# One transposed form of the tokens for both attentions, and router logits from columns of two products, in a transformer block with two attentions and a mixture of experts

## The chip, the cores and the metric

The kernel runs on one core of one Trainium2 chip. The metric is device time in microseconds (us). The engines are PE (TensorE; PEld is its weight load), DVE (VectorE), ACT (ScalarE), POOL (GpSimd) and SP, which here only issues DMAs. Each engine takes its own instructions in the order of the program, and a semaphore holds an instruction back until what it needs is done.

## The reference

The input is x, 32 sequences of 256 tokens of 128 numbers, in float32. The parts that matter:

```
xn = layernorm(x)                                   # no weights
q, k, v = xn @ Wq, xn @ Wk, xn @ Wv                 # attention A: 16 heads of 8, over the 256 tokens
scores = (qc @ kc.T + q_var * k_var) / D            # centred q and k, and their variances
a = softmax(scores) @ v @ Wo
hn = layernorm(xn) * ln1_w + ln1_b                  # attention B: over the 32 sequences, causal
qkv = hn @ in_proj_w.T + in_proj_b
attn = softmax_causal(q @ k.T / sqrt(8)) @ v @ out_proj_w.T + out_proj_b
x1 = xn + attn
hn2 = layernorm(x1) * ln2_w + ln2_b
rp = softmax(hn2 @ router_w.T)                      # 8 experts, the best two
y = sum over the two of gate * gelu(hn2 @ w1[e]) @ w2[e]
out = x + a + x1 + y
```

Note that xn is a layernorm of x, and that hn normalises xn once more: its mean is already zero, and its scale differs from one only through the epsilon. The factor between the two is one number for each token, called r2 in the code.

## The kernel before, in words

**First phase (first_rounds, last_rounds).** Attention B and the router run in 16 chunks of 512 tokens: a chunk is 16 positions of all 32 sequences, as four tiles (k) of 128 tokens. The loop `for i in range(-2, NCHUNK)` works on several chunks at once: turn_in and project_in for chunk i + 2, scores for i + 1, weigh for i, project_out for i - 1, the logits for i - 2. The order of the calls is the order of the instructions on each engine (`manual_schedule`); nothing reorders them.

The steps that the change or the prediction touches:
- load (L140) brings a chunk, in runs of four tokens (2 KB); up to seven chunks are resident.
- stats (L257) takes mean and variance of four tiles on VectorE (L262, L263) and the reciprocal square root on POOL (L265, L266). measure (L269) calls it for the chunk i + 4 and goes on with six small POOL instructions (L274 to L280); the last is r2.
- norms (L288) writes xn to `zx` on ScalarE (L291), and POOL multiplies by r2 for zn (L295).
- turn_in (L303) transposes both xn (pta, into `xnT`, for attention A) and zn (ptb, into hT with ln1's weights, for attention B). POOL then adds the output bias to zx (L311).
- project_in (L313) makes keys (pk, L316), queries (pq, L322) and values (pv, L327), which ScalarE copies out (kb L320, qT L324, v L328). The values go through DRAM (`vald`) and come back in another arrangement (spread, L334).
- scores, lessened (L374, L375 on VectorE: maximum and subtraction, four groups), exponents (L378), turn_weights (ptp, L383), weigh (L395), divide (L412, L413) are the softmax and its product with the values.
- turn_out (pto, L417) and project_out (px, L424): VectorE adds px to zx for x1 (L426) and takes its statistics; POOL adds x1 to the residual (L429), which goes to DRAM (L431). normalise (L433) on POOL writes hn2 without its weights into zx.
- turn_normed and logits (L440 to L449) transpose this once more (ptc), apply ln2's weights, and multiply by the router's matrix (pl) into `lg`.
- set_second (L221) clears tiles on POOL in rounds 3 to 5.

PSUM has two pools of four banks each; a bank is free for the fourth allocation after it.

**Second phase.** Attention A goes in units of 8 steps (step, L942); each sequence's q, k and v come from project (pp, L557), which reads `xnT` with a stride of 32. Beside the first half runs route (L717): the instructions of the softmax over experts and of the positions are handed out a few a step (some, L931), then 128 indirect DMAs of POOL scatter the tokens to their experts' blocks (L801). Then come the experts (L870), and the second half of attention A with the gathering of their results (L894).

The diff touches these functions:

Of the kernel before, what the change touches and what calls it, by code (L numbers as in the profile page):

```python
# [68 lines left out]
def block_kernel(  # L69
# [26 lines left out]
    xv = x.rearrange("s (i c k) e -> i c s (k e)", c=4, k=4)  # L96
# [7 lines left out]
    xnT = cp.tile([P, NCHUNK, 512], F32, name="xnT")  # L104
# [14 lines left out]
    rv = resd.rearrange("s (i c k) e -> i c s (k e)", c=4, k=4)  # L119

    vec = cp.tile([P, 7], F32, name="vec")
    l1w, l1b, l2w, l2b = (vec[:, n:n + 1] for n in range(4))
# [5 lines left out]
    mhalf = cp.tile([P, 4, 1], F32, name="mhalf")  # L128
    wqkv = cp.tile([P, 3, P], F32, name="wqkv")
    wo = cp.tile([P, P], F32, name="wo")  # L130
    inT = cp.tile([P, 3, P], F32, name="inT")
    outT = cp.tile([P, P], F32, name="outT")
    rT = cp.tile([P, NE], F32, name="rT")

# [5 lines left out]
    def load(i):  # L140
        xt = ax.tile([P, 4, P], F32, tag="xt", name=f"xt{i}")
        for c in range(4):
            nc.sync.dma_start(xt[32 * c:32 * c + 32].rearrange("s k e -> s (k e)"), xv[i, c])
        return xt
# [13 lines left out]
    late = xnT[:, NCHUNK - 2:NCHUNK].rearrange("p i t -> p (i t)").rearrange("p (n m) -> p n m", m=P)  # L158
    ipw, opw, qkw, rw, bvs = late[:, 0:3], late[:, 3], late[:, 4:6], late[0:NE, 6], late[:, 7]
    qkT, ccen = zx[:, NTILE - 2:NTILE], zx[:, NTILE - 3]  # L160

    def loads():
# [7 lines left out]
        nc.scalar.dma_start(opw, out_proj_w)  # L170
        nc.scalar.dma_start(bout, out_proj_b.partition_broadcast(P))
# [3 lines left out]
        nc.sync.dma_start(rw, router_w)  # L175
# [5 lines left out]
    def set_in():  # L181
        nc.vector.tensor_scalar(bk4, cst[:, C_M4:C_M4 + 4], bk, None, ALU.mult)
        pt = bank_u([P, 4, P], "pt0")
        for n in range(3):
            nc.tensor.transpose(pt[:, n, :], ipw[:, n, :], ident)
        nc.tensor.transpose(pt[:, 3, :], opw, ident)
        nc.vector.tensor_copy(inT[:, 0:2, :], pt[:, 0:2, :])

        nc.vector.tensor_copy(
            inT[:, 2, :].rearrange("p (j g d) -> p j g d", j=4, g=4),  # L190
            pt[:, 2, :].rearrange("p (g j d) -> p j g d", j=4, g=4),
        )
        nc.vector.tensor_copy(outT, pt[:, 3, :])
# [7 lines left out]
    def set_rest():  # L201
        pt = bank_w([P, 4, P], "pt1")
        nc.tensor.transpose(pt[:, 0, :], qkw[:, 0, :], ident)
        nc.tensor.transpose(pt[:, 1, :], qkw[:, 1, :], ident)
        nc.tensor.transpose(pt[:, 2, 0:NE], rw, ident[0:NE, 0:NE])
        nc.vector.tensor_copy(qkT, pt[:, 0:2, :])
        nc.vector.tensor_copy(rT, pt[:, 2, 0:NE])
# [3 lines left out]
        nc.vector.tensor_copy(wqkv[:, 0:2, :], pb)  # L211

# [42 lines left out]
    xts, rss, nrm, mvs, zns, hTs, qTs, kbt, scs, prs, pTs, wps, os, oTs, x1s, h2s = ({} for _ in range(16))  # L255
# [198 lines left out]
    def first_rounds():  # L454
# [9 lines left out]
        for i in range(-2, NCHUNK):  # L464
# [48 lines left out]
            if chunk(i - 2):  # L513
                turn_normed(i - 2)
# [506 lines left out]
```

## Time and profile before

The time before is 1243.65 us, the median of 15 runs (1237.62 to 1249.68).

| | |
|---|---|
| profiled execution, its own time | 1243.08 us |
| its span, first to last instruction | 1240.9 us |
| mean granted TensorE clock | 0.895 |
| PE, PEld busy | 1014.7, 707.2 us |
| DVE, ACT, POOL busy | 707.8, 659.6, 562.2 us |
| packets of all DMAs | 87,747, of 76.32 MB |

In time: the first phase lasts to about 285 us, its rounds some 14 us each; attention A's first half runs at about 8.5 us a unit until 392; from 392 to 564 all engines but POOL are nearly still, while POOL scatters (384 to 547); then attention A goes on to 742, the experts run until 885, and attention A's second half with the gathering until the end.

How to read the lines: a row of a timeline gives the start, the busy time, the engine, the line of the kernel, the operation, what is written and read, the shape and the count; in brackets stands how long the engine was idle before it, and what released it. PE's rows can overlap, since matmuls are pipelined. A row of stages gives, for each engine, its busy time and in brackets its instructions.

### The profile page before, as it was taken

What the parts mean: (1) busy time and instruction counts of PE and PEld (TensorE: products, weight loads), DVE (VectorE), ACT (ScalarE), POOL (GpSimd) and SP (SyncE); (2) the same over time, 40 slices, a digit from 0 to 9 for tenths busy, and PEclk for the clock granted to TensorE, in tenths of its full rate; (3) what the DMA queues carried; (4) which work ended last, traced back from release to release, by engine and by line L of the source; (5) the groups of instructions that cost most, each with busy time, mean ns of one, the idle gap of its engine ahead of it and who ended that gap; (6) DMA issues with size and microseconds to landing.
All of it is one profiled execution on the core that took longest, in us unless ns stands there. A gap on an engine that the chain in (4) does not pass through costs nothing.

```text
span 1240.9 us, 32300 instructions
## 1 busy us (share of the span) xinstructions
PE 1014.7 (82%) x13107; PEld 707.2 (57%) x13107; DVE 707.8 (57%) x1638; ACT 659.6 (53%) x1362; POOL 562.2 (45%) x725
## 2 busy tenths in 40 slices
PE   5888999889997211008999999999889989899998
PEld 3667777666664000005666659999645555556665
DVE  2576777579996000006888864444455555557883
ACT  4777788736664000004666665555444544446664
POOL 6488887540004777740000003333578888884000
PEclk8898999999998555557999999999979988999999
DMA  3344443203001611110000004444122211110000
GB/s 92 121 136 129 138 136 90 61 20 102 2 2 33 101 52 52 52 63 1 2 2 2 2 13 130 133 133 137 60 64 66 69 37 56 56 52 16 23 10 14
DMA packets 87747, 76.32 MB, mean 61 GB/s; under 512 B 32840, under 2 KB 70864, under 8 KB 87600
## 3 DMA queue, kind: packets, MB, share of 16 engines
q1 hardware_dynamic: 74736, 48.03, 13.7%
q0 software_dynamic: 11600, 26.10, 6.5%
q8 instruction: 103, 1.69, 0.6%
q14 instruction: 44, 0.36, 0.1%
q10 hardware_dynamic: 1264, 0.14, 0.1%
HBM read 33.98 MB, written 40.24 MB: 60 GB/s over the span
## 4 chain that ended last, share of the span: by engine, by line
PE 67%; another core or an unknown queue 15%; DVE 7%; issue 4%; POOL 3%; ACT 3%; DMA 1%; DVEq 0%; SPq 0%; ACTq 0%; POOLq 0%
PE sm L610 19%; PE pav L634 10%; PE pe L854 5%; PE ph L845 5%; PE pp L557 5%; PE sT L616 4%; PE pqk L584 2%; PE pt L653 2%; PE ptp L300 2%; DVE pr L375 1%; PE sc L359 1%; PE px L834 1%; DVE mt L622 1%; DVE mx L374 1%
## 5 line engine op out<-in xcount | busy, mean ns | idle before, releaser
L622 DVE TENSOR_REDUCE mt<-sm 128x2 f32<-128x512 f32 x512 | 329.3, 686 | 295.3 <-remote 190.9
L625 ACT ACTIVATE ex<-sT 128x512 f32<-128x512 f32 x512 | 279.4, 595 | 358.2 <-PE sT L616 160.1
L610 PE MATMUL sm<-ka,qa 32*128 32x256 f32 x2048 | 324.8, 417 | 77.8 <-DVE mt L622 61.0
L616 PE MATMUL sT<-qa,ka 32*128 32x256 f32 x2048 | 323.1, 415 | 48.8 <-issue 40.0
L610 PEld LDWEIGHTS sm<-ka,qa 32*128 32x128 f32 x2048 | 190.0, 191 | 168.2 <-DVE mt L622 88.9
L616 PEld LDWEIGHTS sT<-qa,ka 32*128 32x128 f32 x2048 | 192.4, 191 | 63.7 <-issue 47.7
L634 PE MATMUL pav<-ex,va 128*32 128x256 f32 x2048 | 160.3, 395 | 37.8 <-issue 37.1
L859 POOL DMA_DIRECT2D ysd<-ye x71 | 47.2, 665 | 290.4 <-issue 200.2
L801 POOL DMA_INDIRECT xsd<-zx,posi x128 | 123.2, 963 | 81.3 <-DVE posi L789 42.7
L905 POOL DMA_INDIRECT yg<-ysd,posb x128 | 122.5, 957 | 43.0 <-issue 30.9
L634 PEld LDWEIGHTS pav<-ex,va 128*32 128x32 f32 x2048 | 58.4, 111 | 118.3 <-issue 83.1
L854 PEld LDWEIGHTS pe<-w,ge 128*128 128x128 f32 x568 | 74.5, 191 | 4.2 <-ACT ge L847 0.7
L854 PE MATMUL pe<-w,ge 128*128 128x128 f32 x568 | 74.9, 275 | 0.3 <-ACT ge L847 0.3
L845 PE MATMUL ph<-xT,w 128*128 128x256 f32 x284 | 73.2, 380 | 0.0
L557 PE MATMUL pp<-wqkv,xnT 128*128 128x384 f32 x128 | 67.7, 611 | 5.0 <-issue 4.2
L858 DVE COPY ye<-pe 128x256 f32<-128x256 f32 x71 | 30.1, 424 | 53.5 <-PE pe L854 53.5
L837 ACT ACTIVATE xT<-px,vec 128x256 f32<-128x256 f32 x71 | 40.0, 564 | 36.9 <-PE px L834 36.9
L920 POOL TENSOR_TENSOR res<-res,yg 128x256 f32<-128x256 f32 x64 | 46.6, 728 | 26.8 <-issue 22.0
L374 DVE TENSOR_REDUCE mx<-sc 128x16 f32<-128x512 f32 x64 | 43.4, 678 | 18.8 <-PE sc L359 18.8
L847 ACT ACTIVATE ge<-ph 128x512 f32<-128x512 f32 x71 | 42.4, 597 | 21.0 <-PE ph L845 21.0
L643 ACT COPY oa<-pav 128x256 f32<-128x256 f32 x64 | 24.1, 377 | 55.1 <-remote 44.1
L378 ACT ACTIVATE pr<-pr 128x1024 f32<-128x1024 f32 x32 | 33.9, 1058 | 36.4 <-DVE pr L375 36.4
(170 smaller groups left out, 1670.6 us busy)
## 6 DMA issues: line engine op xcount, KB each, us to landing
xb<-xsd SPq DMA_DIRECT2D x71, 128.0 KB
ysd<-ye POOLq DMA_DIRECT2D x71, 128.0 KB
xsd<-zero SPq DMA_DIRECT2D x10, 852.0 KB
vald<-v SPq DMA_DIRECT2D x16, 288.0 KB
vb<-vald SPq DMA_DIRECT2D x64, 72.0 KB
xt<-in_L_attn_x_dram SPq DMA_DIRECT2D x64, 64.0 KB
resd<-xt SPq DMA_DIRECT2D x64, 64.0 KB
res<-resd SPq DMA_DIRECT2D x32, 128.0 KB
```

What stands on the lines that cost most here:

```text
L374: nc.vector.tensor_reduce(mx, s, AX.X, ALU.max)
L557: nc.tensor.matmul(pp.rearrange("p n m -> p (n m)"), xs_all[:, ti * P:(ti + 1) * P, s], wqkv.rearrange("p n m -> p (n m)"), start=True, st ...
L610: nc.tensor.matmul(sc[:, i, :], qas[u][r:r + 32, i * P:(i + 1) * P], kas[u][r:r + 32, h, :], start=True, stop=True,)
L616: nc.tensor.matmul(sc[:, i, :], kas[u][r:r + 32, h, i * P:(i + 1) * P], qas[u][r:r + 32, :], start=True, stop=True,)
L622: nc.vector.tensor_reduce(mts[y // 8 % 2][:, :, o:o + 1], sc, AX.X, ALU.max, negate=True)
L625: nc.scalar.activation(exs[y], sc, AF.Exp, scale=1.0 / HD)
L634: nc.tensor.matmul(pos[u][32 * j:32 * j + 32, :], vaugs[s % NV][:, ti, 4 * j + 2 * g + h, :], exs[8 * u + 4 * h + j][:, ti, :], start=(h = ...
L801: yield nc.gpsimd.indirect_dma_start(xsd_views[n * NTILE + k], bass.IndirectOffsetOnAxis(ap=posi[:, k, n:n + 1], axis=0), zx[:, k, :], None,)
L845: nc.tensor.matmul(ph[:, f, :], wb[n][0][:, f * P:(f + 1) * P], xT, start=True, stop=True)
L854: nc.tensor.matmul(pe[:, j, :], ge[:, f, j * P:(j + 1) * P], w2b[:, f, :], start=(f == 0), stop=(f == 1))
L859: nc.gpsimd.dma_start(ysd[n * BLK:(n + 1) * BLK].rearrange("(p j) h -> p j h", j=2), ye)
L905: yield nc.gpsimd.indirect_dma_start(yg[s][:, ti, n, :], None, ysd, bass.IndirectOffsetOnAxis(ap=gt["posb"][:, s, ti, n:n + 1], axis=0),)
```

## The change

A transposed copy of zn alone (`znT`) serves both attentions. ln1's weight goes into the projection's weights (inT, inV) and ln1's bias into in_proj's bias. Attention A would need xn; it takes zn instead and multiplies the products by 1 / r2 for each token, `rall`, when it copies them out of PSUM. rall is made by a reciprocal at the end of measure, and is brought into attention A's order of tokens by a transposition and a way through DRAM (scale_back).

The logits no longer take a transposition and product of their own. With P the router's matrix times ln2's weight, the logits are linear in x1, and x1 is xn plus the attention's output plus a bias: the values' product gets eight more columns (zn times P, then times rall), the output's product gets eight more (out_proj times P), and the rest (mean, bias, scale) is put right once for all tokens, by five POOL instructions at the head of route. normalise still writes zx, now half on POOL and half on VectorE. The tiles hold tokens in another order: load and the residual's writes go in runs of one token (512 B), and the positions' and gates' writes in runs of two numbers.

The diff, cut to its core:

```diff
-    xv = x.rearrange("s (i c k) e -> i c s (k e)", c=4, k=4)
+    xv = x.rearrange("s (i k c) e -> i c s k e", c=4, k=4)
...
-    rv = resd.rearrange("s (i c k) e -> i c s (k e)", c=4, k=4)
+    rv = resd.rearrange("s (i k c) e -> i c s k e", c=4, k=4)
...
     def set_in():
-        nc.vector.tensor_scalar(bk4, cst[:, C_M4:C_M4 + 4], bk, None, ALU.mult)
...
-        nc.vector.tensor_copy(inT[:, 0:2, :], pt[:, 0:2, :])
+        pr = bank_u([P, NE], "ptr")
+        nc.tensor.transpose(pr, rw, ident[0:NE, 0:NE])
+        nc.vector.tensor_scalar(inT, pt[:, 0:2, :], l1w, None, ALU.mult)
+        nc.vector.memset(inV[:, 4, :], 0.0)
+        nc.vector.tensor_scalar(
+            inV[:, 0:4, :].rearrange("p j (g d) -> p j g d", g=4),
             pt[:, 2, :].rearrange("p (g j d) -> p j g d", j=4, g=4),
+            l1w, None, ALU.mult,
         )
+        nc.vector.tensor_copy(rT, pr)
+        nc.vector.tensor_scalar(rP, rT, l2w, None, ALU.mult)
+        nc.vector.tensor_tensor(ipb, ipw, l1bs.unsqueeze(1).to_broadcast([P, 3, P]), ALU.mult)
+        nc.vector.tensor_reduce(bz, ipb, AX.X, ALU.add)
+        nc.vector.tensor_tensor(vec[:, 4:7], vec[:, 4:7], bz.rearrange("p n o -> p (n o)"), ALU.add)
+        nc.vector.tensor_scalar(bk4, cst[:, C_M4:C_M4 + 4], bk, None, ALU.mult)
...
     def measure(i):
...
         nc.gpsimd.tensor_tensor(r2, r2, mhalf, ALU.pow)
+        nc.vector.reciprocal(rall[:, 4 * i:4 * i + 4], r2.rearrange("p k o -> p (k o)"))
...
     def turn_in(i):
-        nc.scalar.copy(
-            xnT[:, i, :].rearrange("p (c k s) -> p k c s", c=4, k=4),
-            transposed(tokens(i), "a", i).rearrange("p (k c s) -> p k c s", k=4, c=4),
-        )
-        hTs[i] = a2.tile([P, 512], F32, tag="hT", name=f"hT{i}")
-        nc.scalar.activation(hTs[i], transposed(zns.pop(i), "b", i), AF.Identity, bias=l1b, scale=l1w)
+        nc.scalar.copy(znT[:, i, :], transposed(zns.pop(i), "b", i))
...
     def project_in(i):
...
-        pv = bank_u([P, 4, 4, 32], f"pv{i}")
-        for k in range(4):
-            nc.tensor.matmul(pv[:, :, k, :], hT[:, k * P:(k + 1) * P], inT[:, 2, :], start=True, stop=True)
-        nc.scalar.copy(
-            vs[i % 2].rearrange("p j k g d -> p (j k g) d")[:, :, 0:HD],
-            pv.rearrange("p j k (g d) -> p (j k g) d", d=HD),
-        )
+        for h in range(2):
+            pv = bank_u([P, 5, 2, 32], f"pv{i}_{h}")
+            for k in range(2):
+                o = (2 * h + k) * P
+                nc.tensor.matmul(pv[:, :, k, :], zT[:, o:o + P], inV, start=True, stop=True)
+            nc.scalar.copy(
+                v[:, :, 2 * h:2 * h + 2].rearrange("p j k g d -> p j (k g) d")[:, :, :, 0:HD],
+                pv[:, 0:4].rearrange("p j k (g d) -> p j (k g) d", d=HD),
+            )
+            t = slice(4 * i + 2 * h, 4 * i + 2 * h + 2)
+            nc.vector.tensor_tensor(
+                lg[:, t, :], pv[:, 4, :, 0:NE], rall[:, t].unsqueeze(2).to_broadcast([P, 2, NE]), ALU.mult
+            )
...
     def project_out(i):
...
+        for h in range(2):
+            px = bank_w([P, 2, P + NE], f"px{i}_{h}")
+            for k in range(2):
+                o = (2 * h + k) * P
+                nc.tensor.matmul(px[:, k, :], oT[:, o:o + P], outX, start=True, stop=True)
+            nc.vector.tensor_tensor(
+                x1[:, 2 * h:2 * h + 2, :], px[:, :, 0:P], tokens(i)[:, 2 * h:2 * h + 2, :], ALU.add
+            )
+            l = lg[:, 4 * i + 2 * h:4 * i + 2 * h + 2, :]
+            nc.vector.tensor_tensor(l, l, px[:, :, P:P + NE], ALU.add)
...
-    def normalise(i, eng=nc.gpsimd):
+    def normalise(i, n=2):
...
         for k in range(4):
+            eng = nc.gpsimd if k < n else nc.vector
...
-    def turn_normed(i):
...
-    def logits(i):
...
+    def scale_back():
+        pr = bank_u([NTILE, P], "pra")
+        nc.tensor.transpose(pr, rall, ident)
+        ra = a1.tile([NTILE, P], F32, tag="ra", name="ra")
+        nc.vector.tensor_copy(ra, pr)
+        nc.sync.dma_start(rnd.rearrange("(n c) s -> n (c s)", c=4), ra)
+        nc.sync.dma_start(rpos[:, 0], rnd.rearrange("(i t) s -> t i s", t=P))
+        nc.vector.tensor_scalar(rpos[:, 1], rpos[:, 0], 1.0 / math.sqrt(HD - 1), None, ALU.mult)
...
-            if chunk(i - 2):
-                turn_normed(i - 2)
...
-            if chunk(i - 2):
-                logits(i - 2)
+            if i == NCHUNK - 3:
+                scale_back()
...
-        nc.scalar.activation(sq, pqk, AF.Square, scale=1.0 / math.sqrt(HD - 1))
+        nc.scalar.activation(sq, pqk, AF.Square, scale=rpos[:, 1, ti, s:s + 1])
...
-        nc.scalar.copy(qk[:, :, 0:HD], pqk)
+        nc.scalar.activation(qk[:, :, 0:HD], pqk, AF.Identity, scale=rpos[:, 0, ti, s:s + 1])
...
     def route():
...
+        yield nc.gpsimd.tensor_tensor(
+            t, mvall[:, :, 0:1].to_broadcast(all8), rows[:, 1:2, :].to_broadcast(all8), ALU.mult
+        )
+        yield nc.gpsimd.tensor_tensor(lg, lg, t, ALU.subtract)
+        yield nc.gpsimd.tensor_tensor(lg, lg, rows[:, 0:1, :].to_broadcast(all8), ALU.add)
+        yield nc.gpsimd.tensor_tensor(lg, lg, rsall.to_broadcast(all8), ALU.mult)
+        yield nc.gpsimd.tensor_tensor(lg, lg, rows[:, 2:3, :].to_broadcast(all8), ALU.add)
         yield nc.vector.tensor_reduce(m, lg, AX.X, ALU.max)
...
-            dv = dram.rearrange("s (i c k) u -> c s i (k u)", c=4, k=4)
+            dv = dram.rearrange("s (n c) u -> c s n u", c=4)
```

## The prediction

> **What bounds the kernel now.** I read the page's busy times first, then the busy time by stage, then one round of the first phase in order of time with the chain of waits beside it, and last the later stages. By stage (start:end, then length, PE, PEld, DVE, ACT, POOL busy, granted clock, DMA share, GB/s):
>
> ```profile
> 116.00:172.00 56.00, 52.61 (x1283) 41.08 (x1282) 40.76 (x119) 47.12 (x81) 45.82 (x72) 1.00 0.42 130
> ...
> 570.00:742.00 172.00, 170.46 (x2119) 107.98 (x2112) 137.95 (x291) 114.30 (x271) 0.00 (x0) 0.98 0.01 2
> ```
>
> The first line is four rounds of the first phase. PE looks like the bound (52.6 of 56), and the change takes matmuls away. But a busy share does not say what ends a round. One round in order of time does:
>
> ```profile
> 161.83 0.69 DVE L426 TENSOR_TENSOR x<-px,zx 128x512 f32<-128x512 f32 x1 [2.94 <-PE px L424]
> ...
> 164.34 0.23 POOL L265 TENSOR_SCALAR rsc<-mvc 128x4 f32<-128x4 f32 x1 [2.18 <-DVE mvc L263]
> ...
> 165.75 0.18 DVE L263 BATCH_NORM_AGGREGATE mva<-sta 128x2 f32<-128x6 f32 x1
> ...
> 165.85 0.66 DVE L374 TENSOR_REDUCE mx<-sc 128x16 f32<-128x512 f32 x1
> ...
> 166.91 1.04 POOL L295 TENSOR_TENSOR zn<-zx,r 128x512 f32<-128x512 f32 x1
> ...
> 167.92 0.23 POOL L265 TENSOR_SCALAR rsa<-mva 128x4 f32<-128x4 f32 x1
> ...
> 170.72 1.04 POOL L280 TENSOR_TENSOR r<-r,mhalf 128x4 f32<-128x4 f32 x1
> ...
> 171.14 0.42 DVE L413 TENSOR_TENSOR o<-po,aden 128x256 f32<-128x256 f32 x1
> ...
> 174.56 1.16 PE L424 MATMUL px<-outT,oT 128*128 128x128 f32 x8
> ...
> 175.83 0.69 DVE L426 TENSOR_TENSOR x<-px,zx 128x512 f32<-128x512 f32 x1 [2.94 <-PE px L424]
> ```
>
> From L426 at 161.83 to L426 at 175.83 is one round, 14.0 us, and the chain of waits runs through it without a gap: VectorE alone from 161.83 to the end of L413 at 171.57 (x1, stats, four softmax groups, two divides), then PE 171.62 to 175.72 (half of pto, pk, pq, pv, px). Call the end of L413 **D**. VectorE's order is the program's: the last stats(i+4) ends at 165.75, its very next instruction is L374. And POOL finishes r, the last value of measure, only at 170.72 + 1.04 = 171.76, because it waits for mvc (164.24), and then has rsc, xt and zn ahead of rsa. Today nothing on VectorE waits for r.
>
> The second attention (second stage line) is PE back to back, 170.5 of 172.
>
> **The change part by part.**
>
> *The wait.* The diff puts a VectorE reciprocal of r2 at the end of measure(i+4). It is queued right behind stats(i+4) and ahead of normalise, both lessened(i+1, 0..1), divide and the rest of the round. The source, r2, is 7.52 us behind the end of mvc (164.24 to 171.76); stats(i+4) cover 1.69 of these. So VectorE stands idle about 5.8 us a round, in the middle of the chain that already sets the round. Who waits behind it: exp of those scores on ScalarE, ptp and pto on PE, and through px the next round.
>
> New round, measured from D:
> - D to the end of px: 4.15 today. pv has 160 columns for 128 (0.89 x 160/128: +0.22), px 136 for 128 (+0.06). 4.43.
> - x1 in two halves (a 128x256 add from PSUM follows in 0.34 by L413; before 0.72 for the whole), lg adds 0.10 each by L449, stats: mvc ends at 6.75 (today 6.67). The lg multiplies and the first half fall into the 2.94 that VectorE waits for px.
> - POOL to r: +7.52 = 14.27. zn also needs ScalarE's norms, which end 9.19 after D (180.76); pv copied in two pieces adds 0.10, still a tie with xt.
> - reciprocal 0.2, two normalise (now VectorE) at 0.27 (L436's four there took 1.15): 15.05.
> - from L374 at 165.85 to 171.57: 5.72, less lg's copy 0.10. Next D at 20.7.
>
> So 20.7 us with a warm PE, not 14.0. On top, PE goes idle: after weigh its next work, ptp, needs the exp of scores that come late, a hole of some 7 us. The row for such a hole (start, busy, then idle before):
>
> ```profile
> 245.88 2.08 PE L424 MATMUL px<-outT,oT 128*128 128x128 f32 x8 [2.50 <-ACT oT L417]
> 247.75 1.68 PE L300 MATMUL ptp<-cst,pr 128*128 128x128 f32 x8
> 249.26 1.03 PE L347 MATMUL sc<-causalb,identb 128*128 128x512 bf16 x4
> ```
>
> px takes 2.08 for 1.06: half clock for 3.4 us. In the start-up the same lasts from 38.14 to 44.0, 5.9 us. In the new round ptp starts 1.85 before D; half clock to 1.55 after D costs the pto-pk-pq-pv-px leg 0.75, half clock to 4.15 after D costs 2.05. The two rows differ and the hole is of neither's length, so I take the middle: 1.35. **Round: 22.0 us** (20.7 to 22.7).
>
> [...]
>
> *Rounds 1 to 11.* Before: first L374 of round 0 at 48.22, that of round 11 at 209.41: 161.2. After: 11 x 22.0, plus set_second's memsets, which stand between xt and zn on POOL (91.73 to 94.20 twice, 124.88 to 126.00 once: 6.1). 248.1. **+87.**
>
> *Start.* In set_in VectorE gets nine more instructions of 0.1 to 0.55 and waits for pbo before measure(1); by rows of like shape 2.6 us, and POOL (start-up's chain) passes it on. Round -1: lessened(0,0) came at 34.25; now it waits for r of chunk 3, 39.6 + 2.6, so 42: +7.8. Round 0: r of chunk 4 was 4.9 behind the first L374 (53.2 for 48.2) with the shift of the round before on top: 61.4 for 48.22. **+13.**
>
> *Rounds 12 to 15.* No measure, but normalise on VectorE waits for rsc and its pow (1.4) and adds 0.54; ptp's second half now needs the bank of pq, free only after qT (one bank more for pv). Round 12 also starts cold: +2, round 13: +1. **scale_back** in round 13: transpose, copy 0.2, write to DRAM, read back, then a VectorE multiply that waits for it, with lessened(14,2) behind it. The write of vald took 2.02 to land; two of these plus two issues of 0.4 plus the hops: 5.5, none of it hidden, since VectorE is the chain here (240.6 to 244.2); 3 if some is. Round 15 +0.5. **+9.**
>
> *Last rounds.* ptc 0.44 and 0.85, pl 0.81 and 0.79, h 0.68, lg 0.10 lie on the chain between 263 and 284 and go: -3.7; two lg adds and split x1 give 0.2 back. **-3.5.**
>
> *What costs nothing.* pta, ptc, pl (0.49 + 0.59 + 0.99 of PE a round), xnT's and h's copies (0.47 + 0.80 of ScalarE), two normalise off POOL (1.6): all lie beside the chain, before and after; if the VectorE wait were not there, they would be worth something. The scale operands of sq, qk and va (nearest: L591 0.49 for L565 0.38, so 0.1 each) lie on ScalarE, which waits 56 of 172 us for PE in the second attention. Token rows of 512 B for 2 KB: four times the packets in loads with a chunk and more of lead. The positions' writes: in 398 to 418 the queue took 41.5% of 16 engines for 16,035 packets, 8.3 ns of an engine each; 12,300 more are 6 us, while SP waits until 547.7 for the scatter anyway. The five POOL steps of the route run ahead of VectorE, a unit early. The stretch 392 to 564, where every engine crawls while POOL scatters, has the same 128 scatters; where it starts moves, its length I take as equal, +-10.
>
> **Sum:** 87 + 13 + 9 - 3.5 = 105.5 on the profiled execution's 1243.1 (span 1240.9 and 2.2 around it; the median of the runs is 0.6 above): **1349 us.**
>
> **Rivals.**
> 1. *PE is cold through the whole round.* The leg ptp to px all at half clock: px ends 8.6 after D for 4.4, round 24.9, 11 x 2.9 = +32: 1381. For it: 7 us of idle in 22. Against: both rows above warm within 6 us of work.
> 2. *The extra VectorE work only.* The wait is mostly covered, POOL reaching r early (it loses 1.6 us of normalise). Rounds 14.0 + 0.2 + 0.5 - 0.1, 14 of them +8, with +9 and -3.5 from above: 1257; up to 1300 if rsa ran before xt and zn. Against: POOL idles before mvc already; its length behind mvc is what counts, and that is untouched.
> 3. *Faster: PE is the bound after all.* PE loses 2.07 and gains 0.28 a round, 13.2 busy to 11.4. Rounds could drop to about 13.0 (12 of them, -12), the tail -3.5, scale_back hidden: 1228. It decides only if VectorE's wait for r ends within the 2.94 it now waits for px, that is if r came 3 us or more earlier than it does. Against: the wait is queued behind stats, after px, not before.
>
> **How the numbers follow.** Forecast 0.73, rival 1 0.10, rival 2 0.12, rival 3 0.05. The forecast's bounds: warm PE -14, start and scale_back 5 less, tail 3 less, scatter stretch +-10; late warm-up +8, scatter +10. From 1318 to 1376 leaves out rivals 2 and 3 and the upper part of rival 1. 0.2% is about what a measurement of this kernel can tell from no change; faster 0.04, within 0.01, slower 0.95.
>
> **What would show it.** Right: VectorE's reciprocal in measure with 5 to 6 us of idle before it, released by POOL's pow (r2), in each of some twelve rounds; L426's halves 21 to 23 us apart; px rows of 1.1 and more after a PE hole; granted clock in the first phase well below 1.00; one 5 us wait of VectorE for rpos by DMA. The second attention keeps 8.5 us a unit. Wrong: rounds of 14 to 15 (rival 2 or 3), or reciprocals that wait under 2 us; a scatter stretch that is longer or shorter than 172 by tens would break the sum elsewhere.

## The result, and the profile after

The changed kernel takes **1365.95 us** (median of 9 runs, 1361.41 to 1370.78), the kernel before 1242.29 us (47 runs). The ratio is **1.0993, 95% interval 1.0972 to 1.1015**. The profiled execution took 1369.86 us, with a span of 1368.1. The forecast was 1349, with a range of 1318 to 1376: the direction and the main wait are as forecast, and the time lies 17 above the forecast.

From the page of the changed kernel: the busy times, and of the 40 slices the granted clock and the share of the DMA engines.

```profile
PE 1037.6 (76%) x12861; PEld 712.0 (52%) x12861; DVE 741.6 (54%) x1759; ACT 658.3 (48%) x1346; POOL 544.4 (40%) x700
...
PEclk9776676867788998565559999999987999999999
DMA  3323123221113007951110000244412211211000
```

PE has fewer instructions and is busy for longer than before (1037.6 us for 1014.7). The clock row goes with it: from the second slice to the eleventh, which lie in the first phase, the digits are 6 to 8; the mean over the whole is 0.846, for 0.895 before. In the DMA row, mark the 7, 9 and 5 in the middle: such a stretch comes up again in the experiments.

By stage (start:end, length, then PE, PEld, DVE, ACT, POOL busy, granted clock, DMA share, GB/s):

```profile
116.00:172.00 56.00, 33.87 (x637) 25.48 (x635) 23.63 (x79) 25.92 (x48) 23.96 (x44) 0.72 0.23 73
172.00:228.00 56.00, 34.30 (x871) 25.46 (x870) 26.40 (x93) 23.34 (x43) 26.09 (x44) 0.74 0.26 82
```

In the same 56 us that held 1283 matmuls before there are 637. No engine is busy for more than 62% of it, and the clock is 0.72. A stage in which everything is half idle is a ring of waits, not an engine that is full.

The round in order of time, D (the end of the second divide, L452) at 212.10:

```profile
211.68 0.42 DVE L452 TENSOR_TENSOR o<-po,aden 128x256 f32<-128x256 f32 x1
...
213.15 1.92 PE L347 MATMUL pk<-znT,inT 128*128 128x512 f32 x2
...
217.43 1.09 PE L466 MATMUL px<-outX,oT 128*128 128x136 f32 x8
...
218.34 0.67 ACT L363 COPY v<-pv 128x256 f32<-128x256 f32 x2
...
218.77 0.45 DVE L368 TENSOR_TENSOR lg<-pv,rall 128x16 f32<-128x16 f32 x2 [5.34 <-ACT v L363]
...
219.13 0.41 DVE L467 TENSOR_TENSOR x<-px,zx 128x256 f32<-128x256 f32 x1
...
221.46 0.18 DVE L300 BATCH_NORM_AGGREGATE mvall<-stc 128x2 f32<-128x6 f32 x1
...
221.73 0.23 POOL L301 TENSOR_SCALAR rsall<-mvall 128x4 f32<-128x4 f32 x1 [13.01 <-DVE mvall L300]
...
228.10 1.04 POOL L316 TENSOR_TENSOR r<-r,mhalf 128x4 f32<-128x4 f32 x1
...
229.17 0.18 DVE L317 RECIPROCAL rall<-r 128x4 f32<-128x4 f32 x1 [5.84 <-POOL r L316]
229.26 0.76 DVE L482 TENSOR_SCALAR zx<-x,mvall,rsall 128x128 f32<-128x128 f32 x2
229.84 0.68 DVE L413 TENSOR_REDUCE mx<-sc 128x16 f32<-128x512 f32 x1
...
233.77 1.97 PE L337 MATMUL ptp<-cst,pr 128*128 128x128 f32 x8 [6.83 <-ACT pr L417]
...
234.91 0.42 DVE L452 TENSOR_TENSOR o<-po,aden 128x256 f32<-128x256 f32 x1
...
236.38 1.13 PE L347 MATMUL pk<-znT,inT 128*128 128x512 f32 x2
...
239.29 1.09 PE L466 MATMUL px<-outX,oT 128*128 128x136 f32 x8
...
242.21 0.41 DVE L467 TENSOR_TENSOR x<-px,zx 128x256 f32<-128x256 f32 x1
```

The next D is at 235.33: the round is 23.2 us, for 14.0. Read it backwards. L413 stands behind the reciprocal, which stood idle for 5.84 us until POOL's r; r ends 7.50 after mvall; mvall comes from x1; and x1 stands behind the two lg multiplies, which wait for ScalarE's copies of the values. The last matmul of px had ended at 218.52. PE, which waits 6.4 to 6.8 us for the late softmax, begins both rounds at half clock (ptp takes 1.97 us each time, at a granted clock of 0.50, for 1.04 at 218.36, at 1.00). How long that lasts differs: pk takes 1.92 in the round shown and 1.13 in the next, where px ends at 240.38, 5.05 after its D for 6.42. But x1 starts 7.03 and 6.88 after D, nearly the same, since the lg multiplies wait for ScalarE either way.

Two rows of the waits (engine, line, releaser: us in total, times, longest) carry the difference:

```profile
DVE rall L317 <- POOL r L316: 92.4, 16, 8.3
...
DVE lg L368 <- ACT v L363: 77.8, 17, 5.9
```

The whole change lies in the first phase. Its last x1 starts at 273.28 in the trace of before and at 401.19 after, 127.9 later; the span grew by 127.2.

### The profile page after: what moved, and what is told of

Read it like the earlier page. It is cut to its first block, busy times and chain, and to the rows that moved or that the text cites. A ratio compares the mean times of both kernels' runs of the same rounds, so it can differ in the third digit from the quotient of the medians.

```text
span 1368.1 us, 31838 instructions
## 1 busy us (share of the span) xinstructions
PE 1037.6 (76%) x12861; PEld 712.0 (52%) x12861; DVE 741.6 (54%) x1759; ACT 658.3 (48%) x1346; POOL 544.4 (40%) x700
## 3 DMA queue, kind: packets, MB, share of 16 engines
q1 hardware_dynamic: 99648, 48.09, 14.8%
q8 instruction: 101, 1.65, 0.5%
## 4 chain that ended last, share of the span: by engine, by line
PE 55%; DVE 11%; another core or an unknown queue 10%; issue 7%; POOL 7%; ACT 6%; DMA 0%; DVEq 0%; POOLq 0%; ACTq 0%
PE sm L650 17%; PE pav L674 9%; PE pe L902 5%; PE ph L893 4%; PE sT L656 4%; PE pp L596 4%; DVE pr L414 2%; ACT kb L351 2%; DVE mx L413 2%; PE pqk L624 2%; DVE mt L662 2%; PE pt L693 2%; PE px L882 1%; DVE zx L482 1%
## 5 line engine op out<-in xcount | busy, mean ns | idle before, releaser
L650 PE MATMUL sm<-ka,qa 32*128 32x256 f32 x2048 | 333.5, 423 | 81.2 <-DVE mt L662 61.1
L656 PE MATMUL sT<-qa,ka 32*128 32x256 f32 x2048 | 328.1, 420 | 57.9 <-ACT ex L665 43.7
L650 PEld LDWEIGHTS sm<-ka,qa 32*128 32x128 f32 x2048 | 194.5, 193 | 173.4 <-DVE mt L662 90.1
L656 PEld LDWEIGHTS sT<-qa,ka 32*128 32x128 f32 x2048 | 195.5, 193 | 74.4 <-ACT ex L665 51.8
L337 PE MATMUL ptp<-cst,pr 128*128 128x128 f32 x256 | 50.5, 355 | 91.7 <-ACT pr L417 89.5
L337 PEld LDWEIGHTS ptp<-cst,pr 128*128 128x128 f32 x256 | 40.1, 184 | 96.0 <-ACT pr L417 91.7
L301 POOL TENSOR_SCALAR rsall<-mvall 128x4 f32<-128x4 f32 x16 | 3.7, 234 | 203.5 <-DVE mvall L300 203.5
L596 PE MATMUL pp<-wqkv,znT 128*128 128x384 f32 x128 | 69.6, 626 | 6.8 <-issue 4.2
```

Of the source, the lines that this page charges most:

```text
L337: nc.tensor.transpose(pt[:, k, :], src[:, k, :], ident)
L596: nc.tensor.matmul(pp.rearrange("p n m -> p (n m)"), xs_all[:, ti * P:(ti + 1) * P, s], wqkv.rearrange("p n m -> p (n m)"), start=True, st ...
L650: nc.tensor.matmul(sc[:, i, :], qas[u][r:r + 32, i * P:(i + 1) * P], kas[u][r:r + 32, h, :], start=True, stop=True,)
L656: nc.tensor.matmul(sc[:, i, :], kas[u][r:r + 32, h, i * P:(i + 1) * P], qas[u][r:r + 32, :], start=True, stop=True,)
```

## The experiments

**The theories.** T: the reciprocal behind the stats, waiting for POOL's r, is the main cost (some 65 to 95 us of the 128); the lg multiply that waits for ScalarE, the half clock of PE, and the rounds behind the measures make up the rest. The rival R: without the new wait for r little would be won, because the new multiplies, ScalarE or PE would set the round near 22 us anyway.

The chips of these runs differ. In the first comparison the kernel before took 1242 us; on the next three chips it took 987.6, 990.8 and 991.1; on the last one 1241.5. So ratios are taken only between runs on one chip. The first phase can be compared across chips: its last x1 starts at 401.19 in the first trace of the changed kernel and at 402.27 on another chip. Totals in the expectations that are reckoned from 1243 are read as differences. "Last x1" below is the start of chunk 15's x1, and a mean round that from chunk 0 to chunk 11 (before: 14.7; after: 23.75); it holds the rounds that set_second's memsets make longer, which the rounds of the expectations mostly leave out.

### The reciprocal alone, put into the kernel before

```diff
+    rall = cp.tile([P, NTILE], F32, name="rall")
...
         nc.gpsimd.tensor_tensor(r2, r2, mhalf, ALU.pow)
+        nc.vector.reciprocal(rall[:, 4 * i:4 * i + 4], r2.rearrange("p k o -> p (k o)"))
```

Nothing reads rall here; the output is unchanged.

> The kernel before with one thing of the change alone: the VectorE reciprocal of r2 at the end of measure, into a tile that nothing reads. Theory (VectorE's wait for POOL's r2 sets the round, and a cold PE lengthens the leg behind it): rounds of about 22 us for 14, start-up about 10 later, 1335 to 1345 us in all, 11 to 12 reciprocals with 5 to 6 us of idle before them. Rival (the round is long because of VectorE's other new work and its wait for ScalarE's copy of the values): under 1255 us.

Measured: 1081.25 us beside 987.58, ratio 1.0929 (1.0891 to 1.0967): +93.7. Last x1 at 367.22, +93.9. VectorE's timeline of this kernel, then its waits:

```profile
210.41 0.18 DVE L264 BATCH_NORM_AGGREGATE mva<-sta 128x2 f32<-128x6 f32 x1
216.46 0.18 DVE L282 RECIPROCAL rall<-r 128x4 f32<-128x4 f32 x1 [5.87 <-POOL r L281]
216.56 0.66 DVE L376 TENSOR_REDUCE mx<-sc 128x16 f32<-128x512 f32 x1
```

```profile
DVE rall L282 <- POOL r L281: 103.9, 16, 12.0
```

Sixteen instructions of 0.18 us cost 93.7 us: not their own 2.9 us, but 5.87 us a round of standing in front of L376. The mean round is 21.9 for 14.7: px comes later here too, 4.9 to 6.5 after D for 4.15, and the mean granted clock of the run is 0.933, for 0.975 to 0.984 in the kernel before on this chip. T is shown in one line of code; the remaining 34 us of the first phase come with the other parts of the change.

### The reciprocal late, and the lg multiply first

From the changed kernel, one edit each and both together. The reciprocal moves to project_in of the same chunk, two rounds later in the order; and the multiply is issued ahead of ScalarE's copy of the same PSUM tile:

```diff
-        nc.vector.reciprocal(rall[:, 4 * i:4 * i + 4], r2.rearrange("p k o -> p (k o)"))
+        r2s[i] = r2
...
     def project_in(i):
         zT = znT[:, i, :]
+        nc.vector.reciprocal(rall[:, 4 * i:4 * i + 4], r2s.pop(i).rearrange("p k o -> p (k o)"))
```

```diff
+            t = slice(4 * i + 2 * h, 4 * i + 2 * h + 2)
+            nc.vector.tensor_tensor(
+                lg[:, t, :], pv[:, 4, :, 0:NE], rall[:, t].unsqueeze(2).to_broadcast([P, 2, NE]), ALU.mult
+            )
             nc.scalar.copy(
...
-            t = slice(4 * i + 2 * h, 4 * i + 2 * h + 2)
-            nc.vector.tensor_tensor(
...
```

> The changed kernel with the reciprocal moved from measure to project_in, two rounds later, where r2 is long done. Theory: the 5.8 us of idle go, PE stays warm; what is late next is the multiply of the logits' columns, which waits for ScalarE's copy of the same bank until 6.3 us after the second divide; rounds of 17 to 18 us, 1285 to 1305 us. Rival (the wait for POOL only hides the other waits): rounds of 20 or more, above 1330 us.

> The changed kernel with the logits' multiply issued ahead of ScalarE's copy of the same bank, the reciprocal left in measure. Theory: px, at half clock, ends only 0.6 us before the multiply now gets through, so the wait for ScalarE is nearly covered: rounds shorter by 0.5 to 0.8 us, 1356 to 1361 us. Rival (that wait is the larger part): shorter by over 2 us a round, 1340 us or less.

> Both edits: the reciprocal two rounds later and the logits' multiply ahead of ScalarE's copy. Theory: with a warm PE px ends 4.5 us after the second divide, so now the second edit is worth 2 to 3 us a round: rounds of 14.7 to 15.4 us, 1255 to 1270 us. Rival (the two edits add up as they do alone): recip_late less 7 us.

| first phase | last x1 | mean round | whole, beside 987.58 | ratio (interval) |
|---|---|---|---|---|
| reciprocal late | 335.38 | 18.65 | 1097.37 | 1.1110 (1.1069 to 1.1151) |
| lg first | 381.46 | 22.12 | 1144.28 | 1.1575 (1.1534 to 1.1617) |
| both | 306.0 | 16.35 | 1068.01 | 1.0812 (1.0772 to 1.0851) |

The late reciprocal takes 66 us off the first phase, lg first 20 alone and 29 on top. R falls: the late reciprocal alone takes away half of the 128 us, and both together 95. The single rounds came out otherwise than expected:

- Reciprocal late: a mean round of 18.65, for 17 to 18.
- lg first alone: 1.6 shorter, for 0.5 to 0.8, and over 2 by the rival. The expectation has px end 0.6 before the multiply gets through; from round to round px ends 5.05 to 6.46 after D, so that this distance differs. With lg first x1 starts 4.6 to 6.2 after D, as soon as the first half of px is there.
- Both: 16.35, for 14.7 to 15.4. The first two rounds take 15.1, with px at full clock (it ends 4.23 after D). From the sixth on ptp or pk runs at half clock again (1.97 us for ptp at 200.29, 1.83 for pk behind it, where 1.04 and 1.02 are the times at full clock), px ends 5.2 to 5.7 after D, and the rounds take 16.7 to 17.2.

VectorE with the reciprocal late, and then with lg first:

```profile
208.04 0.17 DVE L348 RECIPROCAL rall<-r 128x4 f32<-128x4 f32 x1
213.31 0.45 DVE L371 TENSOR_TENSOR lg<-pv,rall 128x16 f32<-128x16 f32 x2 [5.10 <-ACT v L366]
```

```profile
206.54 0.17 DVE L364 TENSOR_TENSOR lg<-pv,rall 128x16 f32<-128x16 f32 x1 [2.55 <-PE pv L362]
207.08 0.17 DVE L364 TENSOR_TENSOR lg<-pv,rall 128x16 f32<-128x16 f32 x1 [0.37 <-PE pv L362]
207.55 0.42 DVE L467 TENSOR_TENSOR x<-px,zx 128x256 f32<-128x256 f32 x1 [0.29 <-PE px L466]
```

In the first, the reciprocal waits for nothing, and the round ends in the wait for ScalarE. In the second the multiplies are released by PE's pv itself, and x1 by px. The two instructions read different columns of the same PSUM tile. In the changed kernel's order VectorE's read waits until ScalarE's read has ended: 5.34 us of idle in the round shown, until 218.77, although the last matmul of pv had ended at 217.59. Why it waits is not shown.

With the reciprocal late alone the round still ends in this wait; without the wait, it falls by another 2.3.

### A repeat, and the positions in rows

The rest of the span, after the last x1, showed something else: it is 759 to 760 us in the three kernels above, and 713 in the kernel before with the reciprocal. The suspect are the positions' and gates' writes, in runs of 8 B for 32. The changed kernel again, and with these writes as the tile lies (512 B a partition), read back in four pieces:

```diff
-    posd = dp.tile([NB, SEQ, 2], I32, name="posd")
+    posd = dp.tile([4, NB, NTILE, 2], I32, name="posd")
...
-            dv = dram.rearrange("s (n c) u -> c s n u", c=4)
-            for c in range(4):
-                nc.sync.dma_start(dv[c], src[32 * c:32 * c + 32])
+            nc.sync.dma_start(dram.rearrange("c s n u -> (c s) n u"), src)
...
```

> The changed kernel itself, beside the others of this call. Theory: the last x1 of the first phase at about 401 us, as in its profile, 128 us after the kernel before's. On a chip where the scatter doesn't stop the other engines, the positions' writes add a stop of some 35 us of their own and the whole is 165 to 180 us over the kernel before; where it does, 120 to 128 over. Rival (the positions' writes cost nothing anywhere): 115 to 130 over on any chip.

> The changed kernel with positions and gates written to DRAM as they lie (512 B a partition) instead of in runs of two numbers; only the reading is in runs of 8 B, as it was. Theory: first phase as in the changed kernel; where the scatter alone doesn't stop the other engines, 35 to 48 us less than the changed kernel, and no stop of all engines in the stretch of the positions' writes; where it does, within 5 us of it. Rival (the remainder comes from ScalarE's scale operands and the later route): within 5 us on any chip.

Measured beside 990.79: the repeat 1162.62, ratio 1.1763 (1.1705 to 1.1820), which is +172, not +124 as on the first chip; in rows 1124.32, ratio 1.1362 (1.1313 to 1.1410), 38.3 less. Two stretches of the repeat and one in rows (stages), and SP's issues of posd; the gates' writes are issued from 561.29 on in the repeat:

```profile
520.00:570.00 50.00, 47.81 (x534) 29.40 (x527) 38.23 (x80) 29.70 (x68) 26.79 (x28) 0.93 0.88 38
570.00:605.00 35.00, 6.69 (x58) 4.43 (x60) 5.23 (x13) 4.38 (x11) 21.49 (x23) 0.58 0.89 85
```

```profile
529.21 13.35 SPq L843 DMA_DIRECT2D posd<-posi  x4
```

```profile
570.00:605.00 35.00, 35.00 (x450) 22.30 (x442) 29.44 (x62) 25.28 (x58) 26.70 (x28) 1.00 0.16 54
```

```profile
529.32 0.34 SPq L841 DMA_DIRECT2D posd<-posi  x1
```

In the repeat's second stretch the 16 DMA engines are 89% busy and PE does 6.69 us of work in 35; in rows PE is busy for all of it. The busy DMA engines alone do not explain it: in the first stretch they are 88% busy and PE works for 47.81 of 50. The repeat's waits show the standstill:

```profile
PEld sm L650 <- issue: 58.1, 125, 28.5
```

The longest single wait is 28.5 us, and it is for nothing that the profile shows; in rows the longest of this kind is 0.4. The four issues of posd took 2.70 us of SP in the trace of before, 13.35 here and 0.34 in rows. So the small runs do cost, some 38 us, on this chip; by what way they stop PE is not shown. After the last x1 the kernel in rows still takes 719.5 us (758.1 in the repeat, 713 in the kernel before with the reciprocal on another chip); these 6 us were not taken apart. On the first chip the time after the last x1 is the same before (1240.9 - 273.3 = 967.6) and after (1368.1 - 401.2 = 966.9): there both kernels stand still for a long stretch anyway while POOL scatters (PE has 25.75 us of work in the 172 from 392 on before, and 16.57 in the 120 from 600 on after), and it looks as if the writes vanish in it; the writes in rows were not run there.

### The clock of PE: two tries

PE's granted clock is 0.50 in its 7 us hole (226.94 to 233.77) and in ptp behind it. If that and the wait for ScalarE cover each other, taking one away wins little. The first try keeps PE busy by doing the weigh of a second half eight times (the same results, seven times for nothing), without and with lg first:

```diff
-        for k in range(2):
-            for g in range(4):
+        for _ in range(8 if h == 1 and i <= 11 else 1):
+            for k in range(2):
+                for g in range(4):
...
```

> The changed kernel, with the matmuls of weigh's second half issued eight times over in the rounds up to 12 (each writes the same values again), so that PE is busy for some 6 us in the hole ahead of ptp. Theory: px comes at full clock, but the logits' multiply still waits for ScalarE's copy, so rounds shorter by 0 to 0.7 us, the whole by 0 to 8. Rival (the half clock is what makes the round longer than 21): shorter by 1.5 to 2.5 us a round, 17 to 28 in all.

> The same repeated matmuls, with the logits' multiply ahead of ScalarE's copy. Theory: now neither covers the other; rounds of 20.5 to 21 us, the last x1 of the first phase at 362 to 370 us (381 with the multiply ahead alone, 401 in the changed kernel). Rival (the clock plays no part): 378 to 384, as with the multiply ahead alone.

It failed as an experiment: 1228.96 beside 990.79, ratio 1.2410 (1.2355 to 1.2465), and 1213.22, 1.2236 (1.2174 to 1.2297). PE's timeline of the first:

```profile
215.56 1.31 PE L435 MATMUL po<-vb,pT 128*32 128x36 f32 x128 [1.49 <-issue]
219.84 2.15 PE L435 MATMUL po<-vb,pT 128*32 128x36 f32 x128 [2.97 <-issue]
...
223.56 1.97 PE L337 MATMUL ptp<-cst,pr 128*128 128x128 f32 x8
```

The small matmuls come in bursts of 128 with 1.5 to 3 us between them in which PE waits for nothing that the profile shows. They last 13.6 us (from 210.02 to 223.62), hold up the divide, and ptp takes 1.97 us again. It says nothing of the clock.

The second try has six matmuls of 128x512 on constant data into the same bank, ahead of weigh's second half, in rounds 1 to 12, overwritten by it:

```diff
+        pb = bank_u([P, 512], f"po{i}_{h}")
...
+        if h == 1 and i <= 11:
+            for _ in range(6):
+                nc.tensor.matmul(pb, inT[:, 0, :], znT[:, 0, :], start=True, stop=True)
```

> The changed kernel with six 128x512 matmuls of constant tiles ahead of weigh's second half in rounds 1 to 12, into the same bank, some 5 us of PE at full clock in the hole ahead of ptp (12 instructions a round for the 900 of the repeated weigh, which came in bursts with gaps). Theory: px comes at full clock, but the logits' multiply still waits for ScalarE's copy of the values; rounds shorter by 0 to 0.7 us for 23.2, the whole by 0 to 8 against the changed kernel (on a chip with the kernel before at 988 to 991: 1155 to 1163). Rival (the half clock alone is what makes the round longer than 21): 17 to 28 less.

> The same fill, with the logits' multiply issued ahead of ScalarE's copy. Theory: neither covers the other any more; rounds of 20.5 to 21 us, the last x1 of the first phase at 362 to 370 us (381 with the multiply ahead alone). Rival (the clock plays no part): 378 to 384.

Beside 991.13: the fill alone 1168.60, ratio 1.1770 (1.1730 to 1.1810), last x1 403.56: nothing gained. With lg first 1136.23, 1.1431 (1.1384 to 1.1478), last x1 370.75, mean round 21.4. The fill alone, a stage and a round of it, and the stage with lg first:

```profile
172.00:228.00 56.00, 44.82 (x836) 28.04 (x834) 27.02 (x95) 23.34 (x44) 25.63 (x42) 0.86 0.26 82
```

```profile
211.95 1.09 PE L337 MATMUL ptp<-cst,pr 128*128 128x128 f32 x8
...
216.12 1.09 PE L470 MATMUL px<-outX,oT 128*128 128x136 f32 x8
...
219.37 0.45 DVE L368 TENSOR_TENSOR lg<-pv,rall 128x16 f32<-128x16 f32 x2 [5.18 <-ACT v L363]
```

```profile
172.00:228.00 56.00, 45.16 (x775) 29.35 (x774) 33.30 (x107) 30.30 (x55) 22.11 (x34) 0.94 0.31 93
```

With the fill, ptp and pk run at full clock (1.09 and 1.02 us), px is done at 217.21, and lg still waits to 219.37, 2.2 us longer, for ScalarE. In the changed kernel px, late by the half clock, ended 0.25 before lg in the round shown, and up to 1.5 before it in others. Two waits lie side by side, and the one for ScalarE ends last: the half clock costs nothing while it stands, and once it is gone, filling the hole wins some 11 us (381.46 to 370.75). Without memsets and with PE warm the rounds are 20.2 to 20.8, as the theory has it; in three rounds pk still runs at half clock (1.89 us at 199.14, for 1.02), and the last x1 comes 0.75 later than expected.

### All mends together

The reciprocal late, lg first, rows, and two more edits: normalise entirely on POOL, as before, and scale_back's multiply moved from round 13 to round 15.

```diff
-    def normalise(i, n=2):
+    def normalise(i, n=4):
...
-        nc.vector.tensor_scalar(rpos[:, 1], rpos[:, 0], 1.0 / math.sqrt(HD - 1), None, ALU.mult)
...
+                nc.vector.tensor_scalar(rpos[:, 1], rpos[:, 0], 1.0 / math.sqrt(HD - 1), None, ALU.mult)
```

> The changed kernel with every found cost mended: reciprocal in project_in, the logits' multiply ahead of ScalarE's copy, all four pieces of normalise on POOL as before, scale_back's multiply in round 15, positions written as they lie. Theory: VectorE's chain is back to 13.9 us a round, with PE's hole ahead of ptp adding up to 1 when it falls to half clock; last x1 at 275 to 290 us (273 before), the whole 0 to 20 over the kernel before. Rival (the change saves PE work and PE is the bound once the waits are gone): 10 to 25 below the kernel before.

1009.13 beside 991.13, ratio 1.0177 (1.0147 to 1.0207); last x1 285.69, mean round 15.3. The two new edits took 20.3 us off the first phase (306.0 to 285.69): 10 in the rounds to chunk 11 and 10 behind it. The theory's ranges hold (last x1 at 275 to 290, 0 to 20 over). The rival, that the work taken away would now show as a gain of 10 to 25, falls. Of the 18 us, 12.4 lie ahead of the last x1; the time behind it is 721, for the 713 of the kernel before with the reciprocal on another chip, and this rest was not taken apart. A round is still half a microsecond longer than before; ScalarE and PE in it:

```profile
186.75 0.70 ACT L358 ACTIVATE qT<-pq,vec 128x512 f32<-128x512 f32 x1
...
187.51 0.66 PE L339 MATMUL ptp<-cst,pr 128*128 128x128 f32 x4 [1.60 <-ACT qT L358]
...
188.00 1.03 PE L389 MATMUL sc<-causalb,identb 128*128 128x512 bf16 x4
```

The second half of ptp takes the bank of pq, since pv now needs one more, and ScalarE copies qT behind four copies of keys; the scores stand behind ptp. So the last edit makes the queries first:

```diff
+        pq = bank_u([P, 512], f"pq{i}")
+        nc.tensor.matmul(pq, inT[:, 0, :], zT, start=True, stop=True)
+        qTs[i] = a2.tile([P, 512], F32, tag="qT", name=f"qT{i}")
+        nc.scalar.activation(qTs[i], pq, AF.Identity, bias=bq, scale=1.0)
         pk = bank_w([P, 512], f"pk{i}")
...
-        pq = bank_u([P, 512], f"pq{i}")
...
```

> This is the kernel with all mends (reciprocal late, lg multiply ahead of ScalarE's copy, normalise all on POOL, scale_back's multiply in round 15, positions written as they lie), with one more edit: project_in makes queries ahead of keys, on TensorE and on ScalarE. In the mended kernel a round took about 15.4 us, and the second half of ptp waited 1.6 us for qT, because the pair of pv tiles takes one bank more and ptp's third bank is that of pq; qT is copied behind four keys' copies. Theory (this wait is what the round has too much): with queries first the wait goes, the scores come 0.8 to 1.2 us earlier in a round, the rounds fall to some 14.3 to 14.7, and the whole lies 10 to 16 us below the mended one's 18 above the kernel before: 2 to 8 us above the kernel before of this chip. Rival A (the keys are the bound: the scores need pk's bank, which is free only after the last key, and the keys now end 0.6 us later behind the queries): rounds of 15.0 to 15.4 and 14 to 20 us above. Rival B (the work taken away now counts): below the kernel before by 3 to 10 us.

1254.58 beside 1241.48, on a chip like the first: ratio 1.0094 (1.0059 to 1.0129), +13.1. Last x1 280.40, mean round 14.8. PE in this kernel:

```profile
182.12 1.04 PE L339 MATMUL ptp<-cst,pr 128*128 128x128 f32 x8
182.99 0.81 PE L389 MATMUL sc<-causalb,identb 128*128 128x512 bf16 x3
184.32 0.38 PE L389 MATMUL sc<-causalb,identb 128*128 128x512 bf16 x1 [0.52 <-ACT kb L358]
```

All of ptp goes in one piece, as the theory has it. But the last of the four score tiles now waits for the keys, as rival A has it, and so the rounds lost 0.5 us and not 0.8 to 1.2. The mean round of 14.8 and the +13.1 lie between the two expectations. This run and that of the mended kernel lie on chips of different kinds, so between them only the first phase compares. No version that was run beats the kernel before.

## Why the prediction was right

**The wait.** Predicted: r 7.52 after mvc, VectorE idle 5.8 us a round, in the chain. Measured 7.50 and 5.84: right to the tenth. That the wait is the main cost is shown by the reciprocal alone, +93.7. From L413 to the next D 5.62 was predicted, 5.49 measured.

**Start.** +13 predicted, the first softmax group of round 0 at 61.4; measured at 61.54, +13.3. Right.

**Rounds 1 to 11.** +87 predicted (248.1 us from round 0's first group to round 11's); measured 322.58 - 61.54 = 261.0, +99.8. Without the memsets a round takes 23.1 to 23.4, above the 20.7 to 22.7 that was given. The step that failed is the one that puts x1 after D: "The lg multiplies and the first half fall into the 2.94 that VectorE waits for px." They don't: they wait for ScalarE's two copies of pv, 77.8 us in all (a part of which VectorE would have waited for px anyway), and in all eleven rounds x1 starts 6.9 to 7.2 after D, where the prediction had 4.5 warm and 5.9 with its middle value for the clock. This makes the 1.1 us a round. The middle value itself, 1.35 us, did not fail: px ends 5.05 to 6.46 after D, 5.96 in the mean of the eleven, 1.53 over the warm 4.43. But it decided nothing, since lg's wait ended later in every one of these rounds: with the fill px ends 4.2 to 4.5 after D in nine of them, and x1 still starts 6.9 to 7.2 after D. So the prediction had the wait for r right, and put the wrong wait beside it. A row of before has the pattern:

```profile
392.49 0.48 DVE L592 TENSOR_SCALAR ka<-pqk,cst 128x256 f32<-128x256 f32 x1 [1.32 <-ACT ka L591]
```

Two engines read one PSUM tile, and the second in the program waits for the first although the data are long there: ScalarE's starts at 391.98, VectorE's at 392.49 after 1.32 us of idle, and the matmuls of pqk had ended at 388.87. These two also write halves of one tile, ka, so this row alone doesn't say which of the two sets the order; the lg multiply and the copy of v share only the PSUM tile.

**Rounds 12 to the end.** +9 and -3.5 predicted; measured 401.19 - 322.58 = 78.6 for 63.9, +14.7. The mis-sized term is that normalise on VectorE "adds 0.54". Two rows of the changed kernel:

```profile
357.67 1.55 DVE L482 TENSOR_SCALAR zx<-x,mvall,rsall 128x128 f32<-128x128 f32 x2 [1.49 <-POOL rsall L302]
...
366.49 0.20 DVE L494 TENSOR_SCALAR rpos<-rpos 128x64 f32<-128x64 f32 x1 [3.72 <-DMA rpos<-rnd]
```

The wait of 1.4 was right (1.49), but the two instructions take 1.54 to 2.29 in rounds 12 to 15, for the 0.54 predicted and the 0.76 of the steady rounds (the last section shows beside what). For scale_back 5.5 was predicted, and 3 if some of it is hidden; its wait was 3.72, in the place that was named. Taking both away won 10 us behind chunk 11, in the mended kernel; how the +14.7 divides among normalise, lg's wait and the half clock at the start of rounds 12 and 13 (ptp takes 1.97 us after holes of 2.38 and 3.30) was not taken apart. A part of the -3.5 lies behind the last x1, so the two sides of this comparison do not meet exactly.

**What costs nothing.** On the first chip the time after the last x1 changed by less than 1 us, inside the +-10 that was given. But "The positions' writes" were priced by the share of the queue (6 us, hidden), and on another chip they cost 38 us, with PE standing still beside them: right only for the chip of the trace. On that other chip the whole change costs +172, where the range amounts to +75 to +133; that the measured time lies in the range is to this extent luck of the chip. No run shows a gain from the removed matmuls and copies: with the new waits mended that were found, the kernel is still 1.8% (interval 1.5 to 2.1) and 0.9% (0.6 to 1.3) slower than before. But these kernels have waits and longer stretches of their own, so it isn't shown that the removed work is worth nothing.

**The sum.** 13 + 87 + 9 - 3.5 was 105.5; measured 13.3 + 99.8 + 14.7 = 127.8 to the last x1. Both misses, 12.8 in the rounds to 11 and 9.2 behind them, go the same way. The bounds that are listed add up to 1317 and 1367; no term gives the other 9 us up to 1376, and the measured 1365.95 just does without them. **Rival 1** (cold for the whole round, 24.9) was too long: pv and px ran at full clock at the end of the leg (1.25, 1.09; the granted clock is 1.00 from 216.10). **Rival 2** asked for a covered wait, **rival 3** for an r that came 3 us earlier; the 5.84 us speak against both.

**The half clock.** It lasts from ptp at 210.54 into pq (1.65 us for 1.02 at full clock), to about 216.1, some 5.6 us; in the next round from 233.77 only into pk (1.13), to about 236.6, some 2.8 us. (Estimates: the ends are reckoned from how late the next product starts.) The granted clock agrees: 0.50 from 210.54 to 215.07 and 1.00 from 216.10 to 218.50; 0.50 from 233.77 to 235.70 and 1.00 from 236.60 to 240.40. The two rows of before, 3.4 and 5.9, lie in about the same spread, so a middle value was a fair choice. Nor is the last hole alone what counts: in the kernel with both edits, ptp at 200.29 takes 1.97 us after 1.24 us of idle, and in the one with the fill and lg first ptp at 218.26 takes 1.10 after 1.95. What sets the length is not shown.

## What to carry to other kernels

Before adding a small instruction to an engine that carries the chain, ask what its source is and what stands behind it: sixteen reciprocals of 0.18 us cost 94 us by their place, and wait for nothing two rounds later in the same queue. Where a second engine begins to read a PSUM tile, look for its wait: here it waited for the engine that reads first in the program (77.8 us in all), and putting the short read first took 20 us off. Of two waits that lie side by side, taking away the one that ends first shows nothing, though it was worth 11 us once the other was gone; so take away the one that ends last before saying that a cost is free. And read such an overlap from several rounds: one round showed the two waits 0.25 us apart, others 1.5.

## What the runs showed of the hardware that was not expected

**The chips of these runs differ in how far the scatter disturbs the rest.** The same kernel before takes 988 to 991 us on three chips, and 1242 in the first comparison and on the last chip. POOL scatters at the same pace, an instruction each 1.25 us, but on one kind the other engines nearly stand still. The kernel with queries first on a chip of the slower kind:

```profile
460.00:500.00 40.00, 7.57 (x13) 2.46 (x12) 0.00 (x0) 0.00 (x0) 30.55 (x32) 0.50 0.15 52
```

Thirty-two of POOL's instructions in 40 us, and PE, VectorE and ScalarE issue 13 between them. In the rows' 570 to 605 shown above, on the other kind, POOL does 28 in 35 us and PE is busy throughout. The DMA share is the same (0.15 and 0.16). Why the chips differ was not settled, nor whether it is the chip or its state on that day.

**The DMA engines beside the runs of 8 B.** With the 8 B writes the engines were busy for 0.88 of 50 us that moved 38 GB/s, and for 0.89 of the next 35; in rows that second stage runs at 0.16 and 54 GB/s. PE worked through the first (47.81 of 50) and stood still in the second (6.69 of 35), on a chip where the scatter alone doesn't stop it (35.00 of 35 in rows). In the trace of before, with runs of 32 B, the queue took 41.5% of the engines between 398 and 418, while the positions were written and read back.

**VectorE beside POOL.** normalise's tensor_scalar of 128x128 on VectorE takes 0.42 us in the median of 34, and 1.30 at most. The long ones (339.09, 357.67, 377.54, 392.76 and 405.17) run beside a tensor_tensor on POOL, which starts 0.06 or 0.07 before them, and ends at 358.87 here:

```profile
357.60 1.27 POOL L474 TENSOR_TENSOR xt<-xt,x 128x512 f32<-128x512 f32 x1
```

VectorE's two from 357.67 above take 1.55, to 359.22; those from 339.09 take 2.29, to 341.38, beside two tensor_tensor on POOL, the second of which ends at 341.30. Those from 229.26, beside POOL's own tensor_scalar, take 0.76. Whether the instruction waits for POOL's tensor_tensor, no run tests.
